# Two-layer metaformer block: the combine, norm and transposes of the routed experts done by halves of the tokens, and the last slot's Gelu in two parts

## The chip, the cores and the metric

The kernel runs on one core of a Trainium2 chip. All data are fp32. The metric is the device time of one execution in microseconds; the time of a version is the median of its runs. A profile is one further execution, recorded by the hardware.

The engines are named as in the profile: PE does matmuls (PEld loads their weights), DVE does vector operations, ACT does activations (it has to load a table set before a function that the present set lacks), POOL does vector operations and the indirect DMAs, SP issues most DMAs. Each engine works through its own queue in the order that was fixed when the kernel was built.

## The reference

The input x has 4 batches of 384 channels and 32 x 32 positions (1024 tokens). Two layers follow each other, each with a convolution-like part and a token part:

```
x = x + scan_block(ln_c(x))            # selective scan in 4 directions, norm, gelu
t = tokens(x)
t = t + experts(ln_t(t))               # 4 experts, top 2 per token:
                                       #   scores -> softmax -> top 2, weights masked / sum
                                       #   h = gelu(x @ w1[e] + b1[e]);  y = h @ w2[e] + b2[e]
                                       #   out = sum over the two experts of weight * y
x = from_tokens(t)
x = x + attention(ln_c(x))             # 8 heads of 64, q = k = v = one projection
t = tokens(x)
t = t + ffn(ln_t(t))                   # Kronecker weights, gelu
```

The change touches the gelu of the experts, the sum `t + out`, and the norm `ln_c` (mean and variance over the 384 channels of each token, eps 1e-6) with which the attention begins.

## The kernel before, in words

`build` runs the scan layer for batches 0 to 3. When batch b of the scan is traced, `between` traces the "tail" of batch b - 1: routing, experts, attention and the last layers. So tails 0 to 2 share the engines with the scan of later batches; the tail of batch 3 comes last, with the tail of batch 2 finishing beside its experts. From its attention on, batch 3 is alone.

The order of work on each engine isn't written out by hand. The framework traces the program, gives each instruction a priority by its place in the program, and fills each engine's queue in a simulated time: at each moment the ready instruction with the best priority. A block under `high_priority(offset=FORWARD)` (FORWARD = 20000) is moved that far forward; `combine` and `prologue` stand in such a block, `experts` and `attention` don't. `depend` adds a dependency by hand, `issue_after` keeps an instruction behind another on its engine. Buffers are handed out by tags with a fixed number of slots: in PSUM, tag "p" has 3 banks and tag "o" has 1 in all stages up to the attention of batch 3, which has 6 and 2.

**Scan.** Per unit of 512 tokens and 128 channels, POOL multiplies (L440, L468), ACT takes the exponential (L449, into PSUM), DVE scans (L454) and multiplies (L461), PE sums over states (L475). SP loads its operands (`dtr` L424, `bcs` L350). For batches after the first POOL has L395 and L396 as well.

**Experts.** The 2048 (token, expert) rows of a batch lie sorted by expert in 11 slots: 8 of 256 rows, 3 of 128. Per slot the rows are transposed (L924), h is made in chunks of one PSUM bank (L941; in a slot of 128 rows a chunk holds 4 of the 12 blocks of 128 hidden units), ACT moves each block to `hs` with its bias (L946, Identity), then one Gelu works on the whole of `hs` in place (L949) and `exp_again` puts the log/exp table set back behind it (L148). PE multiplies by w2 (L956, `y_ps` in bank "o"), DVE adds the bias (L960), a DMA writes the rows (L963; for the last slot on ACT's queue). Each fp32 matmul appears in the profile as two records, a transpose as one.

**Combine.** `xt` (the residual tokens, 8 blocks of 128) is loaded. POOL makes two diagonal matrices of the gate weights (L977) and issues 16 indirect DMAs (L986), two per token block, that fetch the two experts' rows into `got[m]`. For each block PE multiplies by the diagonals (L993, `w_ps` in bank "p") and DVE adds the sum to `xt` (L996). One SP DMA stores `xt` (L997).

**Prologue.** `stats` takes each block's mean and variance on DVE (L543, L544); after all eight, ACT makes the inverse root as exp(-0.5 ln(var + eps)) (L152, L153), copies it to a PSUM bank of tag "p" (L552), DVE makes `less` = -mean * rstd (L553), ACT writes the normed blocks over `got[m]` (L1009, eight). Then, for each half of the tokens and each of 3 channel chunks, PE transposes four blocks into one bank "p" (L1017) and ACT copies it to `xc` (L1021).

**Attention.** Per pair of heads, `project` loads weights (L1035), multiplies by `xc` in two halves of 512 tokens (L1042, copies L1045) and transposes (L1051, copies L1054). Scores (L1065), exponentials (L1071) and their products (L1111) follow in steps of 128 by 512.

Of the kernel before, what the change touches and what calls it, by code (L numbers as in the profile page):

```python
# [11 lines left out]
AF = mybir.ActivationFunctionType  # L12
# [5 lines left out]
P = 128  # L18
B = 4
D = 384  # L20
DC = D // P
HW = 32
L = HW * HW
HF = 512
NH = L // HF
# [12 lines left out]
FC = HID // P  # L38
# [7 lines left out]
NSLOT = NFULL + NHALF  # L46
# [5 lines left out]
MB = L // P  # L52
# [63 lines left out]
class Body:  # L116
# [389 lines left out]
    def first_layer(self, b, room):  # L506

        self.experts(b, self.slots, room)
        with self.tc.high_priority(offset=FORWARD):
            xt, xn = self.combine(b, *self.place, room)  # L510
            return self.prologue(xt, xn, room)

    def second_layer(self, b, xc, room, between):
        att = self.attention(xc, self.sums[:, b], room)
# [18 lines left out]

        return self.x2[b].rearrange("(m p) d -> p m d", p=P)

    def stats(self, xt, eps, room):

        nc = self.nc
        st = room.tile([P, MB, 6], "st", "st")
        mv = room.tile([P, MB, 2], "mv", "mv")  # L540
        rstd = room.tile([P, MB], "rstd", "rstd")
        for m in range(MB):
            nc.vector.bn_stats(st[:, m, :], xt[:, m, :])  # L543
            nc.vector.bn_aggr(mv[:, m, :], st[:, m, :])  # L544
        self.inverse_root(rstd, mv[:, :, 1], eps)
        return mv[:, :, 0], rstd

    def less_mean(self, mean, rstd, room, tag):

        less = room.tile([P, MB], tag, "less")  # L550
        ps = room.bank("p", "less_ps")[:, :MB]
        self.nc.scalar.copy(ps, rstd)  # L552
        self.nc.vector.scalar_tensor_tensor(less, mean, -1.0, ps, op0=ALU.mult, op1=ALU.mult)  # L553
        return less
# [316 lines left out]
    def experts(self, b, routed, room):  # L871
# [60 lines left out]
        for s in range(NSLOT):  # L932
            w1, w2, bb = weights
            at, size = extent(s)
            hs = room.tile([P, FC, size], "k12", "hs")
            n = HF // size
            for f in range(0, FC, n):
                ps = room.bank("p", "h_ps").rearrange("p (r l) -> p r l", l=size)
                for r in range(n):
                    for c in range(DC):  # L940
                        nc.tensor.matmul(  # L941
                            ps[:, r, :], w1[(f + r) // wf][:, c, (f + r) % wf * P : ((f + r) % wf + 1) * P],
                            xc[:, c, :], start=(c == 0), stop=(c == DC - 1),
                        )
                for r in range(n):
                    nc.scalar.activation(  # L946
                        hs[:, f + r, :], ps[:, r, :], AF.Identity, bias=bb[:, f + r : f + r + 1]
                    )
            self.exp_again(nc.scalar.activation(hs, hs, AF.Gelu).ins)  # L949
            if s + 1 < NSLOT:  # L950
                weights, xc = fetch(s + 1), gather(s + 1)
            y = room.tile([P, size // P, D], "k4", "y")
            for t in range(size // P):
                out = room.bank("o", "y_ps")
                for f in range(FC):
                    nc.tensor.matmul(  # L956
                        out[:, :D], hs[:, f, t * P : (t + 1) * P], w2[f // wf][:, f % wf, :],
                        start=(f == 0), stop=(f == FC - 1),
                    )
                nc.vector.tensor_add(y[:, t, :], out[:, :D], bb[:, FC:])  # L960

            queue = nc.sync if s + 1 < NSLOT else nc.scalar
            queue.dma_start(  # L963
                out=made[at : at + size, :].rearrange("(t p) d -> p t d", p=P), in_=y
            )

    def combine(self, b, pos, gate, room):


        nc = self.nc  # L970
# [12 lines left out]
        for m in range(MB):  # L983
            got.append(room.tile([P, TOP, D], "kw", "got"))
            for k in range(TOP):
# [1 line left out]
                    out=got[m][:, k, :], out_offset=None, in_=self.made[b][:, :],  # L987
                    in_offset=bass.IndirectOffsetOnAxis(ap=pos[:, k, m : m + 1], axis=0),
                )
        for m in range(MB):  # L990
            ps = room.bank("p", "w_ps")[:, :D]
            for k in range(TOP):
                nc.tensor.matmul(  # L993
                    ps, diag[k][:, m, :], got[m][:, k, :], start=(k == 0), stop=(k == TOP - 1)
                )
            nc.vector.tensor_add(xt[:, m, :], xt[:, m, :], ps)  # L996
        nc.sync.dma_start(out=self.tokens(b), in_=xt)  # L997
        return xt, [got[m][:, 0, :] for m in range(MB)]

    def prologue(self, xt, xn, room):


        nc = self.nc
        mean, rstd = self.stats(xt, self.eps6, room)
        less = self.less_mean(mean, rstd, room, "less")
        for m in range(MB):
            nc.scalar.activation(  # L1009
                xn[m], xt[:, m, :], AF.Identity, bias=less[:, m : m + 1], scale=rstd[:, m : m + 1]  # L1010
            )
        xc = room.tile([P, DC, L], "k12", "xc")
        for i in range(NH):
            for c in range(DC):
                ps = room.bank("p", "tc_ps")
                for j in range(HF // P):
                    nc.tensor.transpose(  # L1017
                        ps[:, j * P : (j + 1) * P], xn[i * (HF // P) + j][:, c * P : (c + 1) * P],
                        self.ident,
                    )  # L1020
                nc.scalar.copy(xc[:, c, halves(i)], ps)  # L1021
        return xc
# [452 lines left out]
```

## Time and profile before

| | |
|---|---|
| median of 3 runs | 4278.92 us (4278.86 to 4291.83) |
| the profiled execution's own time | 4300.74 us |
| its span, first to last instruction | 4299.0 us |
| mean granted clock of PE | 0.865 |
| busy: PE, DVE, ACT, POOL | 77%, 66%, 59%, 70% |
| last slot's Gelu of batch 3, start | 3968.94 us |
| gathers of batch 3, first and last issue | 3983.42 and 4004.11 us |
| first w_ps of batch 3's attention | 4017.40 us |

A row of the timeline gives the start in us from the span's start, the duration of the group in us, the engine, the line of the kernel, the operation, what it writes and reads, how many instructions are merged, and in brackets the idle time before it with what ended it. A row of the table of stretches gives start and end, length, the busy time of PE, PEld, DVE, ACT and POOL in that stretch with the number of instructions, PE's granted clock (1.00 is full speed), the share of the DMA engines that was busy, and GB/s.

### The profile page before, as it was taken

Reading aid. Unit: us, or ns where it says so; the run is one execution under the profiler, and the core shown is the slowest. Engines: PE = TensorE matmul, PEld = TensorE weight load, DVE = VectorE, ACT = ScalarE, POOL = GpSimd, SP = SyncE. Lnnn points to the kernel's source line nnn. Section 1 sums busy time; section 2 is a strip of 40 time slices with the busy share of each in tenths; the row PEclk is TensorE's granted clock in tenths of the full one; section 3 lists DMA queues with packets and bytes.
Section 4 is the critical chain, followed back from the end, with each engine's and each line's share of the span. In section 5 each row is a group of like instructions: output and inputs, shape, how many; then the busy total and the mean of one; then the engine's idle time right before and its main releaser. Section 6 shows DMA issues by size and latency. Waiting matters only on the chain. (4 is left out here: it accounts for less than half of the span.)

```text
span 4299.0 us, 45575 instructions
## 1 busy us (share of the span) xinstructions
PE 3329.5 (77%) x13244; PEld 1560.8 (36%) x13244; DVE 2852.0 (66%) x4200; ACT 2516.4 (59%) x4486; POOL 3020.0 (70%) x1471
## 2 busy tenths in 40 slices
PE   6445444389897888589985889579896889998896
PEld 2111111155553223145652223135553225566322
DVE  5998997878786867788786878878887820010101
ACT  5555545556665775666664777666665654343354
POOL 5999997898898968789898978888989810000100
PEclk8666666689998999589997999679998999999997
DMA  5454563577795535578886434558789243345100
GB/s 140 128 124 122 135 170 107 168 220 224 229 276 158 137 113 142 169 207 236 239 257 191 114 101 140 158 173 237 234 236 272 77 158 100 121 143 202 50 26 19
DMA packets 410322, 693.69 MB, mean 161 GB/s; under 512 B 51024, under 2 KB 209616, under 8 KB 410064
## 3 DMA queue, kind: packets, MB, share of 16 engines
q1 hardware_dynamic: 400752, 664.29, 53.4%
q0 software_dynamic: 8192, 25.17, 1.8%
q8 instruction: 106, 1.74, 0.2%
q14 instruction: 152, 1.25, 0.1%
q10 hardware_dynamic: 1120, 1.25, 0.1%
HBM read 569.00 MB, written 121.50 MB: 161 GB/s over the span
## 5 line engine op out<-in xcount | busy, mean ns | idle before, releaser
L440 POOL TENSOR_TENSOR bx<-dtr,bcs 128x1024 f32<-128x1024 f32 x768 | 1791.8, 2358 | 181.1 <-PE acc L475 93.6
L449 ACT ACTIVATE da<-dtr,nega 128x512 f32<-128x512 f32 x1536 | 1045.5, 690 | 928.7 <-DVE bx L461 580.8
L468 POOL TENSOR_TENSOR bx<-bx,bcs 128x1024 f32<-128x1024 f32 x384 | 903.7, 2357 | 154.6 <-DVE carry L465 67.3
L475 PE MATMUL acc<-bx,sel 128*32 128x512 f32 x3072 | 493.5, 701 | 306.4 <-POOL bx L468 261.0
L941 PE MATMUL h_ps<-xc,w 128*128 128x256 f32 (+1 forms) x3168 | 663.5, 365 | 47.7 <-DVE xc L928 17.4
L956 PE MATMUL y_ps<-w,hs 128*128 128x384 f32 x1824 | 644.6, 507 | 52.5 <-ACT hs L949 52.5
L941 PEld LDWEIGHTS h_ps<-xc,w 128*128 128x128 f32 x3168 | 551.2, 198 | 218.9 <-issue 93.7
L454 DVE TENSOR_TENSOR_SCAN bx<-da,carry,bx 128x512 f32<-128x512 f32 x384 | 473.8, 1270 | 114.7 <-ACT da L449 64.4
L454 DVE TENSOR_TENSOR_SCAN da<-da,carry,bx 128x512 f32<-128x512 f32 x384 | 476.1, 1273 | 77.5 <-ACT da L449 62.1
L454 DVE TENSOR_TENSOR_SCAN bx<-da,bx 128x512 f32<-128x512 f32 x384 | 453.7, 1211 | 90.9 <-ACT da L449 54.3
L461 DVE TENSOR_TENSOR bx<-da,bcs 128x512 f32<-128x512 f32 x768 | 509.8, 679 | 3.0
L454 DVE TENSOR_TENSOR_SCAN da<-da,bx 128x512 f32<-128x512 f32 x384 | 455.5, 1219 | 76.5 <-ACT da L449 53.0
L956 PEld LDWEIGHTS y_ps<-w,hs 128*128 128x128 f32 x1824 | 353.0, 197 | 337.4 <-issue 71.7
L1071 ACT ACTIVATE ex<-s_ps 128x512 f32<-128x512 f32 x512 | 300.3, 591 | 164.2 <-PE s_ps L1065 148.4
L1065 PE MATMUL s_ps<-w 64*128 64x512 f32 x1024 | 305.1, 659 | 68.5 <-ACT ex L1071 64.4
L977 POOL TENSOR_TENSOR diag<-ident,g_weight 128x1024 f32<-128x1024 f32 x8 | 15.1, 1903 | 443.1 <-PE xc_ps L924 430.0
L1111 PE MATMUL o_acc<-ex,vt 128*64 128x512 f32 x1024 | 286.1, 638 | 24.6 <-ACT ex L1071 18.5
L946 ACT ACTIVATE hs<-h_ps,bb 128x256 f32<-128x256 f32 (+1 forms) x528 | 199.9, 440 | 174.9 <-PE h_ps L941 170.9
L475 PEld LDWEIGHTS acc<-bx,sel 128*32 128x32 f32 x3072 | 76.2, 116 | 603.9 <-POOL bx L468 373.3
L960 DVE TENSOR_TENSOR y<-y_ps,bb 128x384 f32<-128x384 f32 x76 | 41.6, 548 | 250.6 <-PE y_ps L956 250.6
L365 PE MATMUL dt_ps<-xd,wdt 108*128 108x512 f32 x192 | 123.6, 731 | 73.0 <-ACT mag L404 48.3
L1065 PEld LDWEIGHTS s_ps<-w 64*128 64x128 f32 x1024 | 81.8, 189 | 269.1 <-ACT ex L1071 222.6
(218 smaller groups left out, 3593.3 us busy)
## 6 DMA issues: line engine op xcount, KB each, us to landing
w<-in_w SPq DMA_DIRECT2D x352, 576.0 KB
dtr<-dd SPq DMA_DIRECT2D x1536, 128.0 KB
bcs<-both SPq DMA_DIRECT2D x512, 128.0 KB
dd<-one_e SPq DMA_DIRECT2D x96, 256.0 KB
dd<-mag SPq DMA_DIRECT2D x96, 256.0 KB
rows<-zero SPq DMA_DIRECT2D x76, 192.0 KB
xt<-x SPq DMA_DIRECT2D x32, 384.0 KB
xs<-rows SPq DMA_DIRECT2D x32, 384.0 KB
```

Of the source, the lines that this page charges most:

```text
L440: pool = nc.gpsimd.tensor_mul(bx, dtr[q][1], bc[:, 0].unsqueeze(1).to_broadcast([P, 2, HF])).ins
L449: nc.scalar.activation(da, dtr[q][0][:, j, :], AF.Exp, scale=nega[:, col : col + 1])
L454: nc.vector.tensor_tensor_scan(run(h), run(da), run(bx[:, j, :]), 0.0 if first else hold, ALU.mult, ALU.add,)
L461: dve = nc.vector.tensor_mul(bx[:, j, :], h, cg).ins
L468: pool = nc.gpsimd.tensor_mul(bx, bx, cg.unsqueeze(1).to_broadcast([P, 2, HF])).ins
L475: nc.tensor.matmul(acc[lo : lo + DB, :], sel, out[q][:, j, :], start=(g == 0), stop=(g == NG - 1),)
L941: nc.tensor.matmul(ps[:, r, :], w1[(f + r) // wf][:, c, (f + r) % wf * P : ((f + r) % wf + 1) * P], xc[:, c, :], start=(c == 0), stop=(c = ...
L946: nc.scalar.activation(hs[:, f + r, :], ps[:, r, :], AF.Identity, bias=bb[:, f + r : f + r + 1])
L956: nc.tensor.matmul(out[:, :D], hs[:, f, t * P : (t + 1) * P], w2[f // wf][:, f % wf, :], start=(f == 0), stop=(f == FC - 1),)
L1065: ins = nc.tensor.matmul(ps, w[rows, j * P : (j + 1) * P], w[rows, halves(i)], start=True, stop=True).ins
L1071: done.append(nc.scalar.activation(ex[:, o, :], ps, AF.Exp, scale=HD**-0.5, accum_out=sums[:, t, 2 * j + o, i : i + 1],).ins)
L1111: ins = nc.tensor.matmul(out[cols, :], made[t][1][:, j, cols], ex[:, o, :], start=(j == 0), stop=(j == MB - 1),).ins
```

## The change

- **Combine.** The loop over token blocks becomes an inner function `add(m)`, which `combine` returns. The store of `xt` becomes two DMAs, each for four blocks, issued behind blocks 3 and 7.
- **Prologue.** It runs over the two halves. For each half: `add(m)`, statistics of four blocks; inverse root, `less` (for four columns, through the bank "o" in place of "p"); four normed blocks; then the transposes and copies of this half. `xc` is taken from its pool after the first half's norms. `stats` goes away. Another caller, `second_layer_exact`, passes no `add`; it runs only if a guard on the attention's sums is hit.
- **Last slot of the experts.** When PE has done the first matmul of the last block of the last chunk, one Gelu works in place on the 8 blocks of `hs` that the chunks before have filled (it has a hand-made dependency on that matmul). The four blocks of the last chunk go from PSUM through Gelu with their bias straight to `hs`, with no Identity. `exp_again` follows the last of them. Other slots stay as they are.

```diff
@@ -507,8 +507,8 @@
 
         self.experts(b, self.slots, room)
         with self.tc.high_priority(offset=FORWARD):
-            xt, xn = self.combine(b, *self.place, room)
-            return self.prologue(xt, xn, room)
+            xt, xn, add = self.combine(b, *self.place, room)
+            return self.prologue(xt, xn, room, add)
 
     def second_layer(self, b, xc, room, between):
         att = self.attention(xc, self.sums[:, b], room)
@@ -533,22 +533,11 @@
 
         return self.x2[b].rearrange("(m p) d -> p m d", p=P)
 
-    def stats(self, xt, eps, room):
-
-        nc = self.nc
-        st = room.tile([P, MB, 6], "st", "st")
-        mv = room.tile([P, MB, 2], "mv", "mv")
-        rstd = room.tile([P, MB], "rstd", "rstd")
-        for m in range(MB):
-            nc.vector.bn_stats(st[:, m, :], xt[:, m, :])
-            nc.vector.bn_aggr(mv[:, m, :], st[:, m, :])
-        self.inverse_root(rstd, mv[:, :, 1], eps)
-        return mv[:, :, 0], rstd
-
-    def less_mean(self, mean, rstd, room, tag):
-
-        less = room.tile([P, MB], tag, "less")
-        ps = room.bank("p", "less_ps")[:, :MB]
+    def less_mean(self, mean, rstd, room, tag, bank="p"):
+
+        n = rstd.shape[-1]
+        less = room.tile([P, n], tag, "less")
+        ps = room.bank(bank, "less_ps")[:, :n]
         self.nc.scalar.copy(ps, rstd)
         self.nc.vector.scalar_tensor_tensor(less, mean, -1.0, ps, op0=ALU.mult, op1=ALU.mult)
         return less
@@ -935,18 +924,25 @@
             hs = room.tile([P, FC, size], "k12", "hs")
             n = HF // size
             for f in range(0, FC, n):
+                last = s == NSLOT - 1 and f == FC - n
                 ps = room.bank("p", "h_ps").rearrange("p (r l) -> p r l", l=size)
                 for r in range(n):
                     for c in range(DC):
-                        nc.tensor.matmul(
+                        ins = nc.tensor.matmul(
                             ps[:, r, :], w1[(f + r) // wf][:, c, (f + r) % wf * P : ((f + r) % wf + 1) * P],
                             xc[:, c, :], start=(c == 0), stop=(c == DC - 1),
-                        )
+                        ).ins
+                        if last and r == n - 1 and c == 0:
+                            wide = nc.scalar.activation(hs[:, :f, :], hs[:, :f, :], AF.Gelu).ins
+                            self.depend(wide, ins)
                 for r in range(n):
-                    nc.scalar.activation(
-                        hs[:, f + r, :], ps[:, r, :], AF.Identity, bias=bb[:, f + r : f + r + 1]
-                    )
-            self.exp_again(nc.scalar.activation(hs, hs, AF.Gelu).ins)
+                    done = nc.scalar.activation(
+                        hs[:, f + r, :], ps[:, r, :], AF.Gelu if last else AF.Identity,
+                        bias=bb[:, f + r : f + r + 1],
+                    ).ins
+            if not last:
+                done = nc.scalar.activation(hs, hs, AF.Gelu).ins
+            self.exp_again(done)
             if s + 1 < NSLOT:
                 weights, xc = fetch(s + 1), gather(s + 1)
             y = room.tile([P, size // P, D], "k4", "y")
@@ -987,30 +983,45 @@
                     out=got[m][:, k, :], out_offset=None, in_=self.made[b][:, :],
                     in_offset=bass.IndirectOffsetOnAxis(ap=pos[:, k, m : m + 1], axis=0),
                 )
-        for m in range(MB):
+        def add(m):
             ps = room.bank("p", "w_ps")[:, :D]
             for k in range(TOP):
                 nc.tensor.matmul(
                     ps, diag[k][:, m, :], got[m][:, k, :], start=(k == 0), stop=(k == TOP - 1)
                 )
             nc.vector.tensor_add(xt[:, m, :], xt[:, m, :], ps)
-        nc.sync.dma_start(out=self.tokens(b), in_=xt)
-        return xt, [got[m][:, 0, :] for m in range(MB)]
-
-
-
-    def prologue(self, xt, xn, room):
+            if m % (MB // NH) == MB // NH - 1:
+                part = slice(m + 1 - MB // NH, m + 1)
+                nc.sync.dma_start(out=self.tokens(b)[:, part, :], in_=xt[:, part, :])
+
+        return xt, [got[m][:, 0, :] for m in range(MB)], add
+
+
+
+    def prologue(self, xt, xn, room, add=lambda m: None):
 
 
         nc = self.nc
-        mean, rstd = self.stats(xt, self.eps6, room)
-        less = self.less_mean(mean, rstd, room, "less")
-        for m in range(MB):
-            nc.scalar.activation(
-                xn[m], xt[:, m, :], AF.Identity, bias=less[:, m : m + 1], scale=rstd[:, m : m + 1]
-            )
-        xc = room.tile([P, DC, L], "k12", "xc")
+        nh = MB // NH
+        xc = None
         for i in range(NH):
+            st = room.tile([P, nh, 6], f"st{i}", "st")
+            mv = room.tile([P, nh, 2], f"mv{i}", "mv")
+            rstd = room.tile([P, nh], f"rstd{i}", "rstd")
+            for j in range(nh):
+                m = i * nh + j
+                add(m)
+                nc.vector.bn_stats(st[:, j, :], xt[:, m, :])
+                nc.vector.bn_aggr(mv[:, j, :], st[:, j, :])
+            self.inverse_root(rstd, mv[:, :, 1], self.eps6)
+            less = self.less_mean(mv[:, :, 0], rstd, room, f"less{i}", "o")
+            for j in range(nh):
+                m = i * nh + j
+                nc.scalar.activation(
+                    xn[m], xt[:, m, :], AF.Identity, bias=less[:, j : j + 1], scale=rstd[:, j : j + 1]
+                )
+            if xc is None:
+                xc = room.tile([P, DC, L], "k12", "xc")
             for c in range(DC):
                 ps = room.bank("p", "tc_ps")
                 for j in range(HF // P):
```

## The prediction

> **What bounds the kernel now.** I read the granted clock first (0.865 over the 4299.0 us span), then the table of stretches, then the timeline of the one place that the change touches without cover, last the chain that ended last and POOL's waits.
>
> ```profile
> 806.00:3445.00 2639.00, 2154.76 (x8935) 1061.28 (x8933) 2078.62 (x3015) 1716.11 (x3035) 2252.08 (x1098) 0.89 0.65 189
> 3445.00:3966.00 521.00, 494.58 (x2056) 287.57 (x2056) 54.77 (x160) 221.70 (x430) 22.27 (x21) 0.98 0.44 148
> 3966.00:4024.00 58.00, 36.41 (x106) 18.34 (x105) 11.10 (x26) 15.29 (x27) 16.10 (x17) 0.85 0.28 86
> 4024.00:4299.00 275.00, 238.08 (x943) 78.39 (x942) 19.56 (x37) 136.49 (x329) 0.00 (x0) 0.92 0.06 19
> ```
> Columns: stretch, length, busy us of PE, PEld, DVE, ACT and POOL, granted clock, DMA share, GB/s. From 806 to 3445 the scan of one batch and the experts of another share the engines: POOL is busy 85%, PE 82%, nobody is alone. From 3445 to 3966 (rest of batch 2, experts of batch 3) PE is busy 95%. From 3966 to 4024 PE is busy 63%: the end of the last slot, the combine and the prologue of batch 3, with no other work left. After that the attention holds PE; the chain that ended last alternates there between L1065 and L1111. So a microsecond taken from 3966 to 4024 is a microsecond of the time. The same code runs three times more under the scan (last slot, combine, prologue near 1290 to 1358, 2270 to 2328, 3290 to 3355), where it counts only through the other engines.
>
> The uncovered place, by its timeline (start, us, engine, line, count, idle before):
> ```profile
> 3966.48 1.14 ACT L946 ACTIVATE hs<-h_ps,bb 128x128 f32<-128x128 f32 x4 [1.54 <-PE h_ps L941]
> 3967.64 1.28 ACT L949 ACT_TABLE_LOAD   x1
> 3968.94 1.48 ACT L949 ACTIVATE hs<-hs 128x1536 f32<-128x1536 f32 x1
> 3970.47 9.57 PE L956 MATMUL y_ps<-w,hs 128*128 128x384 f32 x24 [4.03 <-ACT hs L949]
> ...
> 4009.30 0.18 DVE L544 BATCH_NORM_AGGREGATE mv<-st 128x2 f32<-128x6 f32 x1
> 4009.51 0.30 ACT L152 ACTIVATE rstd<-mv,eps 128x8 f32<-128x8 f32 x1 [37.80 <-DVE mv L544]
> 4010.54 4.89 ACT L1009 ACTIVATE got<-xt,less,rstd 128x384 f32<-128x384 f32 x8 [0.28 <-DVE less L553]
> 4011.30 2.82 PE L1017 MATMUL tc_ps<-ident,got 128*128 128x128 f32 x12 [3.22 <-ACT got L1009]
> 4015.33 2.96 ACT L1021 COPY xc<-tc_ps 128x512 f32<-128x512 f32 x6
> 4015.95 1.62 PE L1017 MATMUL tc_ps<-ident,got 128*128 128x128 f32 x12 [1.83 <-ACT xc L1021]
> 4017.40 5.32 PE L1042 MATMUL w_ps<-xc,wqkv 128*128 128x512 f32 x12
> ```
> Two stalls: PE idles 4.03 us for the last Gelu; and no norm starts before the eighth token block has its statistics, although ACT had waited 37.8 us. Between them lie the gathers (16 issues on POOL, 1.257 us apart), which set when each block can be added; nothing in the change moves their pace.
>
> **Last slot's Gelu (part A).** Before: four Identities 1.14, table load 1.28, Gelu of 1536 elements 1.48: PE waits from 3966.45 to 3970.47. After: the first 8 of 12 blocks get their own Gelu. From the two L949 forms (3072 elements 2.763 us, 1536 in 1.482) one element costs 0.83 ns and the start 0.20 us, so 1024 elements cost 1.05 us. It waits for a matmul four records before the last: h_ps runs at 4.41/38 = 0.116 us per record, so that one ends at 3966.45 - 0.46 = 3965.99. The table load fits the 1.54 us in which ACT waits for PE anyway, if the wait sits on the Gelu; if the load waits too, it costs 1.28. Wide Gelu 3966.26 to 3967.31, PE starts at 3967.34: 3.1 us sooner (1.85 if the load waits). The four Gelus from PSUM (1.14, as the Identities) end at 3968.45, under the eight y_ps blocks that need only the wide part (16 records of 0.33 us, 5.3 us). The shorter idle has a second effect, which the table of stretches shows:
> ```profile
> 3970.40:3973.70 3.30, 3.23 (x5) 1.85 (x6) 0.00 (x0) 1.30 (x2) 0.00 (x0) 0.51 0.00 0
> 4014.10:4015.90 1.80, 0.02 (x1) 0.00 (x0) 0.00 (x0) 1.80 (x5) 0.00 (x0) 0.85 0.00 0
> 4015.90:4017.40 1.50, 1.45 (x12) 1.33 (x13) 0.00 (x0) 1.50 (x4) 0.00 (x0) 1.00 0.00 0
> ```
> After 4.0 us of idle PE restarts at clock 0.51; after 1.8 us it restarts at 1.00. With an idle of 0.9 us (at most 2.2) y_ps takes 24 x 0.33 = 7.9 instead of 9.57: 1.7 us. Part A: **4.8 us**, low end 3.5.
>
> **Halves (part B), batch 3.** Small instructions added: one more Ln, Exp, copy and less (0.30 + 0.21 + 0.17 + 0.16), all for the first half, at a time when ACT and DVE wait for gathers; the one SP store becomes two of 0.38 us issue, and SP has nothing behind it until 4022.75. The less of the first half makes DVE wait 0.8 us with the adds of blocks 4 to 7 behind it; these come every 2.5 us and cost 1.3, so it is absorbed. Second half: last statistics end at 4009.48 as before, norms start at 4010.54, but four instead of eight: at (4.89 - 0.69)/7 = 0.60 apart the last ends at 4010.54 + 1.80 + 0.69 = 4013.03 (was 4015.43). One transpose (0.135) and one copy (0.58) later, at 4013.85, the second half of w_ps can start; copies two and three (0.475 apart) stay ahead of it. The first half's 12 transposes, 3 copies and 6 of the 12 records of w_ps are done before, in PE's waits (3.22 + 1.83, and those between gathers); its first weights were loaded long before. So w_ps ends at 4013.85 + 6 x 0.443 = 4016.5 instead of 4022.72: **6.2 us**. Low end, 3.0: the queue of PE holds w_ps behind all transposes. Or the 12 first transposes stand ahead of the w_ps of block 4: they end near 4004.6, and blocks 4 to 7 follow at DVE's pace, the last add 1.6 us later: 4.6. High end, 11: v_ps and w_ps of the next head pair (0.6 + 2.7, and a score) fill PE's waits too.
>
> **Batches 0 to 2.** During the 16 gathers POOL does nothing else, and ACT, DVE and PE mostly wait (ACT 20.7 us before L152 at 1347). Moving half of the norms into that time relieves ACT afterwards, but POOL then had work without a gap to 1370, 2340 and 3345. The earlier Gelu hands ACT back to the scan about 2.1 us sooner per batch (ends -6.3 in all); against it stand the new PE and DVE waits in queues that the scan shares. I take 0, with ends -6 and +24 (below).
>
> A rule of the Trainium skill speaks against part A: "ScalarE: Activation LUTs", Table sets, asks to batch activations by table set, since every switch costs some 2.7 us; splitting the Gelu opens a gap into which an Exp of the scan can slip. The trace has that case, at the Gelus of the scan's end:
> ```profile
> 665.90 1.52 ACT L230 ACTIVATE y<-y,cols 128x512 f32<-128x512 f32 x2
> 667.44 1.28 ACT L153 ACT_TABLE_LOAD   x1
> 668.73 0.58 ACT L153 ACTIVATE ln_var<-ln_var 128x512 f32<-128x512 f32 x1
> 669.33 1.28 ACT L230 ACT_TABLE_LOAD   x1
> ```
> Two loads of 1.28 with the next instruction right behind: 2.6 us for each of three batches, 7.7 of ACT at most; by the page, an estimate of 5.3 each, 16. I use the trace's. ACT is busy 65% in that stage, so the wait of POOL behind it, not the sum, would be paid. Batch 3 has no scan and is free of it.
>
> **Sum.** 4.8 + 6.2 + 0 = 11.0 us. The profiled execution took 4300.74 us (span 4299.0, 1.7 around it), so 4289.7 there; it lay 21.8 above the median of 4278.92, and the saved work scales hardly at all, so **4267.9**.
>
> **Rivals.**
> 1. More than forecast: PE's waits take the next pair's work as well (+4.8) and the ACT time freed under the scan reaches POOL (6.3): 4257. For it: project(1) is next in program order and POOL loses 35.4 us to ACT L382. Against: POOL is fully fed right behind each combine.
> 2. The change doesn't do what it says: the planner keeps the first half's transposes and w_ps behind the last block, and its wide Gelu late. Only four fewer norms stay (2.4) with part of A: near 4275. Against: PE's order follows readiness in the planner's simulated time, and in that it has a gap too.
> 3. Slower: under the scan PE's queue now holds transposes that wait for norms, inside the run of gathers and ahead of the L475 matmuls; bx is then released late and POOL stalls. The kind of wait exists:
> ```profile
> POOL bx L440 <- PE acc L475: 83.3, 22, 16.2
> ```
> Single waits reach 16.2 us. It decides from 11.0/3 = 3.7 us per batch; at 8 each, 4278.9 - 11.0 + 24 = 4292. Against: PE was idle in those waits already.
>
> **How the numbers follow.** 0.3% (12.8 us) is about what a measurement of this kernel can tell from no change. Forecast 50%, within 4263 to 4273 (14 of it below 4266.1, faster by over 0.3%; 36 within). Rival 1: 26%, faster. Rival 2: 9%, same. Rival 3: 15%, 13 slower by over 0.3%, 2 same. So faster 0.40, same 0.47, slower 0.13. The range 4254 to 4290 leaves out about 7% below and 9% above.
>
> **What would show it.** A: PE's idle ahead of the last y_ps in batch 3 falls from 4.03 to about 0.9 and the clock behind it stays at 1.00; a load from the log/exp set between the two Gelus of one of batches 0 to 2 shows the skill's rule at work. B: eight norms in two groups of four with the first before the last gather; six w_ps records before the last transposes; last statistics to end of w_ps 7 us instead of 13.2. Wrong if POOL's waits for PE acc between 806 and 3445 grow beyond 83.3 by more than 11, or if the scan ends away from 3445 by more than a few us, since every instruction's place is planned anew.

## The result

The changed kernel takes 4267.69 us (median of 7 runs, 4263.45 to 4277.06), the kernel before 4289.97 in 7 runs beside it (4278.86 to 4292.33; the three shown first are among these). The ratio is 0.9957, 95% interval 0.9942 to 0.9971: about 18 us less, 0.43%. (The two medians are 22.3 us apart, the two means 18.6.) Forecast were 4267.9 us and 11 us less. The number came out; most of the gain did not come from where the forecast has it. "us less" below is the ratio's distance from 1, times 4290, so that experiments made on different chips stand on one scale.

The profiled execution of the changed kernel (4267.69 us, span 4265.9, clock 0.866) against the one shown of before. First the same four stretches, cut at the same events (columns: stretch, length, busy us of PE, PEld, DVE, ACT and POOL, granted clock, DMA share, GB/s):

```profile
799.00:3423.00 2624.00, 2143.28 (x8951) 1060.38 (x8953) 2085.59 (x3015) 1719.87 (x3052) 2251.24 (x1098) 0.89 0.64 190
3423.00:3933.80 510.80, 491.92 (x2041) 288.26 (x2037) 57.27 (x163) 219.93 (x423) 22.76 (x21) 0.98 0.45 151
3933.80:3987.30 53.50, 35.77 (x103) 18.80 (x102) 10.95 (x27) 15.42 (x30) 15.62 (x17) 0.84 0.30 93
3987.30:4265.90 278.60, 241.92 (x943) 79.23 (x942) 19.57 (x37) 136.48 (x329) 0.00 (x0) 0.90 0.06 19
```

The uncovered place of batch 3, third row, went from 57.53 us (3966.45 to 4023.98) to 53.45: 4.1 us where the forecast had 11. The first two rows together are 25 us shorter (2639 + 521 to 2624 + 510.8), where the forecast had nothing; 7 of the 32 us by which the place begins earlier were there before batch 1's scan, at the end of the first stretch of the trace (806 to 799), where both kernels run the same instructions. The last row is 3.6 us longer, with the same instructions. So one pair of executions carries differences of several us that are not the change's.

The timeline of the uncovered place after the change, in the columns of the forecast's second fence:

```profile
3931.17 1.14 ACT L939 ACTIVATE hs<-h_ps,bb 128x128 f32<-128x128 f32 x4 [7.97 <-PE h_ps L931]
3933.45 1.28 ACT L936 ACT_TABLE_LOAD   x1 [1.14 <-PE h_ps L931]
3934.74 1.06 ACT L936 ACTIVATE hs<-hs 128x1024 f32<-128x1024 f32 x1
3935.85 8.01 PE L952 MATMUL y_ps<-w,hs 128*128 128x384 f32 x24 [2.04 <-ACT hs L936]
...
3962.37 12.24 SPq L995 DMA_DIRECT2D x<-xt  x2
3964.20 2.50 ACT L1020 ACTIVATE got<-xt,less,rstd 128x384 f32<-128x384 f32 x4 [0.28 <-DVE less L542]
3964.96 2.82 PE L1028 MATMUL tc_ps<-ident,got 128*128 128x128 f32 x12 [3.21 <-ACT got L1020]
3968.03 5.59 PE L989 MATMUL w_ps<-got,diag 128*128 128x384 f32 x16 [0.25 <-ACT xc L1032]
3974.84 0.18 DVE L1015 BATCH_NORM_AGGREGATE mv<-st 128x2 f32<-128x6 f32 x1
3976.82 2.70 PE L1028 MATMUL tc_ps<-ident,got 128*128 128x128 f32 x12 [3.20 <-ACT got L1020]
3979.31 6.68 PE L1053 MATMUL w_ps<-xc,wqkv 128*128 128x512 f32 x12
```

Three things are to be seen. The table load does not start at 3932.31, when the last Identity had ended, but 1.14 us later, when the matmul that its Gelu waits for was done: it waits with the Gelu. (The wait stands on ACT's queue as an instruction of its own, ahead of the load.) All 16 records of the sums of blocks 4 to 7 (L989) stand behind the first half's 12 transposes (L1028). And all 12 records of the attention's w_ps (L1053) stand behind the second half's transposes; nothing of the attention begins early.

POOL's waits under the scan, from 799 to 3423 (waiting line, releaser: us, times, longest):

```profile
POOL bx L440 <- PE acc L475: 102.1, 33, 15.2
POOL bx L468 <- DVE bx L454: 47.3, 23, 7.3
POOL bx L468 <- DVE carry L465: 43.4, 24, 6.5
```

The wait for PE, 83.3 us before, has grown by 18.8, which the forecast named as a sign that it would be wrong. But all of POOL's waits from 806 to the end of the scan together fell from 374.9 to 360.2 us: POOL waits more for PE and less for others.

### The profile page after: what moved, and what is told of

Its sections match the earlier page's. It is cut to its first block, busy times and chain, and to the rows that moved or that the text cites. A ratio compares the mean times of both kernels' runs of the same rounds, so it can differ in the third digit from the quotient of the medians.

```text
span 4265.9 us, 45621 instructions
## 1 busy us (share of the span) xinstructions
PE 3317.7 (78%) x13244; PEld 1560.6 (37%) x13244; DVE 2863.1 (67%) x4204; ACT 2518.3 (59%) x4498; POOL 3019.6 (71%) x1471
## 5 line engine op out<-in xcount | busy, mean ns | idle before, releaser
L952 PE MATMUL y_ps<-w,hs 128*128 128x384 f32 x1824 | 634.1, 500 | 35.0 <-ACT hs L944 26.6
```

The lines of the kernel that those rows point to most:

```text
L952: nc.tensor.matmul(out[:, :D], hs[:, f, t * P : (t + 1) * P], w2[f // wf][:, f % wf, :], start=(f == 0), stop=(f == FC - 1),)
```

## The experiments

All of these compute the whole of the reference. Five of them need batch 3 to differ from the others; there the functions exist twice, and `b` selects. The planner lays out every queue anew for each build. How far two orders differ is counted here on PE's records in the two traces: like instructions in a row are one run, and a run counts as moved when it has no partner in the other trace's sequence. Before's trace has 1732 runs. (The row counts in the expectations were taken in another, finer way and count both sides of each difference.)

### Which batch gains: the last, or the first three

Both parts of the change in batch 3 alone (`combine_h` and `prologue_h` are the changed functions), so that the queues ahead of it are those of the kernel before (no run of PE or POOL moved up to batch 3's combine):

```diff
+            if b == B - 1:
+                xt, xn, add = self.combine_h(b, *self.place, room)
+                return self.prologue_h(xt, xn, room, add)
...
+                last = b == B - 1 and s == NSLOT - 1 and f == FC - n
```

> Both parts for batch 3 alone; batches 0 to 2 as before, and the queues of the engines up to batch 3's last slot are those of before. The traces of before and after show what the uncovered place gained: the idle ahead of the last y_ps fell from 4.03 to 2.04 us and y_ps took 8.01 instead of 9.57 (part A 3.6), and from the last gather's end to the end of w_ps it went from 17.7 to 17.2 (part B 0.4). So my reading now is 4.0 us less than before. If the forecast's sum for this place is right after all (4.8 + 6.2), it is 11 us less. If the whole gain of the change comes from here, 18 us less.

Measured 0.9993 (0.9983 to 1.0003): 3 us less. The other half of the change, `b < B - 1` in the same two places:

> Both parts for batches 0 to 2 alone; batch 3 as before. Theory 1 (the planner lays the queues anew and happens to do better) and theory 2 (the halves and the earlier Gelu relieve the scan) both expect the rest of the gain here: 18 - 4 = 14 us less than before. The forecast took 0 for these batches.

Measured 0.9941 (0.9927 to 0.9956): 25 us less. So the gain lies in batches 0 to 2, which the forecast took at 0, and batch 3 by itself gives 3 us with an interval that includes nothing.

### Does the order move the time without the change

The kernel before, with its one store of `xt` split in two behind the last block. No computation differs, but from batch 0's combine on (1350 us) the planner then lays PE's queue otherwise: some 620 of its 1732 runs moved:

```diff
-        nc.sync.dma_start(out=self.tokens(b), in_=xt)
+        for part in (slice(0, MB // NH), slice(MB // NH, MB)):
+            nc.sync.dma_start(out=self.tokens(b)[:, part, :], in_=xt[:, part, :])
```

> The kernel before with one edit that does next to nothing: combine's store of xt goes in two DMAs, both after the last block, in all batches. Work added: four issues of 0.38 us on SP. Theory 2 expects no change, within 2 us. Theory 1 expects that this alone has the planner lay the queues of batches 0 to 2 anew and that the time moves by 5 to 20 us, in either direction, with the differences between 800 and 3440 us of the trace.

Measured 1.0071 (1.0053 to 1.0089): 30 us more. One added DMA per batch cost more than the whole change gained. "Both after the last block" holds for the program's text only: each part waits for its own four blocks alone, and in batch 3 the first went out 18.6 us after the end of y_ps, among the gathers.

The same store in four parts (some 65 runs moved, all from batch 2's combine on):

```diff
+        for m in range(0, MB, 2):
+            nc.sync.dma_start(out=self.tokens(b)[:, m : m + 2, :], in_=xt[:, m : m + 2, :])
```

> The kernel before with its x<-xt store in four DMAs behind the last block instead of one. No computation differs; the planner lays 194 rows of TensorE's queue otherwise (two DMAs gave about 1000 rows and 30 us). Theory 1 (order): 3 to 30 us from the kernel before, either way, less than the two DMAs gave if fewer moved rows mean fewer chances. Theory 2 (the issues and the packets of the split store themselves cost): slower than with two DMAs, by 30 to 60 us.

Measured 1.0018 (1.0006 to 1.003): 8 us more. Four DMAs cost less than two, so it isn't the number of DMAs that costs; what goes with the 30 us is the moved order.

The changed kernel, with its store in four parts, one behind every second block (some 280 runs moved, against the changed kernel's 1744):

```diff
-            if m % (MB // NH) == MB // NH - 1:
-                part = slice(m + 1 - MB // NH, m + 1)
+            if m % 2 == 1:
+                part = slice(m - 1, m + 1)
```

> The changed kernel with the store of x<-xt in four DMAs, one behind every second block, instead of two. No computation differs, but the planner lays about 700 rows of TensorE's queue otherwise. Where the store's place alone was changed with all other queues kept, the time stood within 2 us of the changed kernel's. Theory 1 (the gain of batches 0 to 2 belongs to the order that the planner fell into): the time parts from the changed kernel's by 5 us or more, either way. Theory 2 (it belongs to the work by halves): within 4 us of the changed kernel, so 14 to 22 below the kernel before.

Measured 1.0064 (1.0048 to 1.008): 27 us more than before, 46 more than the changed kernel. All of the change's gain in batches 0 to 2 is gone, with the work by halves still there. That is the plainest answer of the study: the work by halves does not bring the gain by itself; with another order of the queues it is gone.

One place where POOL stands is longer in both slow orders. POOL's waits around batch 1's combine and the scan beside it, 2200 to 2600 us, in the kernel before with two stores:

```profile
POOL bx L440 <- PE acc L475: 33.1, 4, 23.2
```

and in the changed kernel with four:

```profile
POOL bx L440 <- issue: 28.4, 3, 22.1
```

One stall of 22 to 23 us each, near 2500 us. ("issue" is time in which nothing that the profile shows was waited for.) The same stall is in the kernel before with 16.2 us (2503) and in the changed one with 14.3 (2462), so it makes 6 to 9 us of the difference; the rest is spread over many waits.

### The two parts, each in all batches

Only the Gelu in two parts (some 330 runs of PE moved, from batch 1's combine on), then only the halves (some 660, from batch 0's):

> The last slot's Gelu in two parts in all batches; sums, norms, transposes and the store as in the kernel before. In batch 3 this is worth 3.5 us by the changed kernel's trace (1.99 shorter idle, 1.56 of clock). In batches 0 to 2 the planner lays about 640 rows of TensorE's queue otherwise, from the end of batch 0 on. Theory 1 (the order that the planner falls into moves the time, whatever the edit): the total is anywhere from 30 us slower to 25 faster, and the trace shows it as POOL's progress through the scan parting from the kernel before at batches 1 to 2, with waits for acc, y or bx grown or shrunk there. Theory 2 (the gain of batches 0 to 2 comes from Gelus that finish earlier): 12 to 25 us faster, with POOL ahead from each batch's last Gelu on.

> Sums, norms, transposes and the store by halves in all batches, the Gelu as in the kernel before. In batch 3 this is worth about 0.4 us by the changed kernel's trace. In batches 0 to 2 about 1050 rows of TensorE's queue are laid otherwise. The change gave 18 us and the Gelu's part alone 2. Theory 1 (the order decides, and no part of the change has its own price in batches 0 to 2): any value from 25 us faster to 30 slower, and the two parts' own gains do not add up to the 18. Theory 2 (the halves are what gained): 14 to 18 us faster, so that with the Gelu's 2 they make the change's 18.

Measured 0.9995 (0.9986 to 1.0005), 2 us less, and 1.0025 (1.001 to 1.0039), 11 us more. Together the parts gave 18 us less; one by one they make 9 more. No price per part can be read from that in batches 0 to 2. In batch 3 the traces add up within 1 us: from the last h_ps to the first score it takes 54.06 us with the Gelu alone (3.47 less than before), 57.66 with the halves alone (0.13 more), and 53.45 with both (4.08 less). But the same code in batch 3 alone took 55.47, for a reason that the section on the hardware shows.

### Batch 3 with the order that the forecast assumed

The change in batch 3 alone once more, with the Gelu's table asked for ahead of its wait, and PE's queue told what the forecast had taken for granted: first half's transposes behind block 5's sum, the first half of the attention's first w_ps behind block 7's, then the second half's transposes. (`done` is the last Identity of the chunk before; `hold` is the matmul behind which the next transposes queue; `first` makes that half of w_ps.)

```diff
+                if last and b == B - 1:
+                    with self.tc.issue_after(done):
+                        nc.scalar.preload_act_table_set("gelu_and_others")
...
+        sums(0)
+        xc = room.tile([P, DC, L], "k12", "xc")
+        sums(1)
+        hold = [self.adds[5]]
+        turn(0)
+        got = first(xc)
+        hold = [got[-1]]
+        turn(1)
```

> As last_only, with the two things mended that cost the forecast its sum in batch 3: the Gelu table set is loaded behind the Identities of the chunk before, and PE's queue has the first half's transposes behind block 5's sum, then, behind block 7's, the first half of w_ps, then the second half's transposes. If the forecast's mechanism was right and only the planner's order was wrong: idle ahead of y_ps 0.9 us, last statistics to end of w_ps 7 us, 11 us less than before. If the places don't pay for another reason (clock, banks), no better than last_only, 4 us less.

Measured 0.9962 (0.9947 to 0.9976): 16 us less. Its timeline:

```profile
3946.81 1.28 ACT L962 ACT_TABLE_LOAD   x1
3948.10 1.06 ACT L971 ACTIVATE hs<-hs 128x1024 f32<-128x1024 f32 x1
3949.21 8.01 PE L987 MATMUL y_ps<-w,hs 128*128 128x384 f32 x24 [0.92 <-ACT hs L971]
...
3975.85 15.58 SPq L1098 DMA_DIRECT2D x<-xt  x2
3983.62 5.49 PE L1092 MATMUL w_ps<-got,diag 128*128 128x384 f32 x8 [4.29 <-DMA got<-made,g_pos]
```

The table load now runs behind the chunk's Identities, PE's idle is 0.92 us and y_ps takes 8.01: part A gives 3.11 + 1.56 = 4.67 us. From the last statistics (3991.84) to the end of the attention's w_ps (3999.24) it takes 7.4 us, against 13.24 before. But PE waits 4.29 us for rows, right after the first half's store went out at 3975.85. The texts on record name block 6; by the count of records, 22 of the 32 stand before this row, so that it is the second expert's rows of block 5, whose gather was issued 0.4 us behind the store.

Is that store to blame? The same kernel with batch 3's store in one DMA at the end, all other queues kept:

```diff
+            if b == B - 1 and m == MB - 1:
+                nc.sync.dma_start(out=self.tokens(b), in_=xt)
+            if b < B - 1 and m % (MB // NH) == MB // NH - 1:
```

> last_fixed with one edit: batch 3's x<-xt store goes out in one DMA behind the sum of block 7 (as in the kernel before) instead of two, the first of them behind block 3. Every other queue is that of last_fixed. Theory 1 (the first half's store of 0.79 MB runs among the last gathers and holds them back): TensorE's wait for got of block 6, 4.29 us in last_fixed, falls to about what the kernel before had there (under 1.5), the sums of blocks 6 and 7 end 2 to 4 us earlier after y_ps, and the time is 2 to 4 us below last_fixed's, so 18 to 20 us below the kernel before by last_fixed's 16. Theory 2 (the gathers of block 6 were late by themselves): the wait stays at 3 to 4.3 us and the time with it, within 1 us of last_fixed.

Measured 0.9976 (0.9966 to 0.9986): 10 us less, so not better than with the early store. The wait in its timeline, though, is gone; the longest for a block is now this one:

```profile
3977.01 0.88 PE L1092 MATMUL w_ps<-got,diag 128*128 128x384 f32 x2 [1.61 <-DMA got<-made,g_pos]
```

Since the two readings disagree, the kernel with the early store was run again:

> last_fixed once more, unchanged, since its time (16 us below the kernel before, 8 runs) and last_late's (10 below, 17 runs) stand in the other order than their traces, where last_late's batch 3 is 3.7 us shorter. Theory 1 (the collision of store and gathers is real and the first median was a lucky one): 7 to 9 us below the kernel before. Theory 2 (the early store is worth its collision for a reason that the traces have not shown): 14 to 18 below again. The trace should again show TensorE waiting some 4 us for got of block 6.

Measured 0.9981 (0.997 to 0.9991): 8 us less, and in this execution the row in question is

```profile
3993.53 4.54 PE L1092 MATMUL w_ps<-got,diag 128*128 128x384 f32 x8 [2.40 <-issue]
```

The uncovered place took 52.22 us in the first execution with the early store, 49.18 in the second, 48.53 with the late one. So the collision costs between 0.7 and 3.7 us in these traces and nothing that the times can tell. Both expectations were too sharp; that a half store among the gathers costs the kernel several us is not shown. The wait itself does follow the store: PE waits for the second rows of block 5 for 4.29 and 2.40 us in these two executions and 1.96 in the kernel before with two stores, and for 0.34 in the kernel before, 0.32 here with the late store and 0.28 in the version with both gains below.

The store's place was also moved in the changed kernel itself:

```diff
-            if m % (MB // NH) == MB // NH - 1:
-                part = slice(m + 1 - MB // NH, m + 1)
-                nc.sync.dma_start(out=self.tokens(b)[:, part, :], in_=xt[:, part, :])
+            if m == MB - 1:
+                for part in (slice(0, MB // NH), slice(MB // NH, MB)):
+                    nc.sync.dma_start(out=self.tokens(b)[:, part, :], in_=xt[:, part, :])
```

> The changed kernel with one edit: both half stores of x<-xt go out behind block 7 in every batch. All queues but SP's are those of the changed kernel, so this is the place of the store alone. Theory 1 (the half store among the gathers holds them and the loads of the scan back by 2 to 4 us a batch, and only batch 3 lies open): 1 to 4 us below the changed kernel, 19 to 22 below the kernel before. Theory 2 (the earlier store of batches 0 to 2 frees SP's queue and was part of the 14 us gained there): 5 to 14 us above the changed kernel.

Measured 0.9952 (0.9936 to 0.9968): 21 us less, as the changed kernel. For batch 3 this was no test: with SP's queue empty, the first store still went out at 3961.61, 26.6 us after y_ps began, as in the changed kernel (26.5), since it waits only for its own four blocks. It serves as a repeat of the changed kernel.

### Both gains together

The changed kernel's batches 0 to 2 with the mended batch 3 and its one late store:

> The change in all batches, its batches 0 to 2 as they stand in the changed kernel, and batch 3 as in last_late (table asked for ahead, the order on TensorE written out, one store). Queues ahead of batch 3 are those of the changed kernel and of early_only. Theory 1 (two gains that add: the queues of batches 0 to 2 as re-planned give what early_only gave, 25 us, and the mended batch 3 gives 12 to 19): 37 to 44 us below the kernel before. Theory 2 (early_only's gain was used up where the batches overlap, so that batch 3's does not add): 20 to 28 us below. The trace should show an idle of 0.9 us ahead of the last y_ps and about 7 us from the last statistics to the end of the attention's w_ps.

Measured 0.9922 (0.9906 to 0.9939), 4253.94 us: 33 us less than before, the best of all versions. It lies between the two expectations, and is about what the two halves measured apart: 25 (batches 0 to 2) and 10 (the mended batch 3). In its trace the uncovered place takes 47.28 us, 10.25 less than in the trace of before.

### All traces side by side

Per profiled execution: the end of POOL's part of the scan, POOL's waits from 806 us to there, the end of the last h_ps of batch 3, the length of the uncovered place (to the first score), and the rest of the span. (The stretches above are cut 11 us behind the end of the scan as it is taken here.)

```
                    less by   scan end  POOL waits  last h_ps  place    rest
queues of before, up to batch 3
  before              -        3434.2     374.9      3966.45   57.53   275.0
  batch 3 alone       3        3421.6     363.4      3943.91   55.47   278.7
  mended, run 1      16        3418.8     364.5      3948.29   52.22   276.6
  mended, run 2       8        3423.7     365.8      3960.04   49.18   272.9
  mended, late store 10        3409.7     353.0      3940.95   48.53   276.8
queues of the changed kernel, up to batch 3
  after              18        3412.0     360.2      3933.81   53.45   278.6
  after, two late    21        3409.0     354.2      3932.99   53.52   279.1
  batches 0 to 2     25        3400.9     347.7      3925.25   60.32   278.7
  both gains         33        3408.9     357.8      3930.30   47.28   274.9
other orders
  Gelu alone          2        3425.4     366.5      3942.20   54.06   274.6
  halves alone      -11        3448.0     391.9      3978.23   57.66   274.8
  before, 4 stores   -8        3441.8     382.8      3980.09   60.90   278.3
  after, 4 stores   -27        3462.1     408.4      3988.86   54.88   274.4
  before, 2 stores  -30        3468.2     412.8      3992.75   60.75   275.0
```

Up to the last h_ps the nine executions of the first two groups fall into two bands that don't overlap: 3941 to 3966 (mean 3951.9) and 3925 to 3934 (mean 3930.6). The distance of the means, 21.3 us, is what the order in batches 0 to 2 is worth by these traces (33, 21 and 9 us between traces taken side by side); 13.9 of it are there when the scan ends, the rest comes while batch 2 finishes beside batch 3's experts. The scan's end follows POOL's waits nearly one to one over all fourteen rows: from 347.7 to 412.8 us of waits (65), from 3400.9 to 3468.2 (67). That is bookkeeping, since POOL is busy for 2250 to 2252 us from 806 to there in all of them: the sum of its waits tells where time goes, and not why.

Where the order helps can be read from POOL's progress. Until batch 0's combine the means of the two bands lie within 5 us; behind it, from POOL's 468th scan product to its 576th, the changed kernel's order gains 18.8 us on average, and behind batch 1's, from the 756th to the 864th, another 23.5, which puts it 39.4 us ahead. By the end of the scan 25.5 of these are given back. Against the mean of the first band slower orders are ahead at the 576th product too, the halves alone by 17 us, the kernel before with two stores by 11 and the changed one with four by 14, the last two behind by 3 and 4 at the 648th; so no single place makes an order good. The second gain by POOL's waits, before (2209 to 2569):

```profile
POOL bx L440 <- PE acc L475: 19.9, 3, 16.2
POOL x L237 <- ACT y L230: 11.8, 2, 9.4
POOL bx L440 <- DMA dtr<-dd: 11.5, 2, 5.9
POOL bx L468 <- DVE bx L454: 10.3, 4, 5.1
```

and after (2194 to 2530):

```profile
POOL bx L440 <- PE acc L475: 22.5, 4, 14.3
POOL x L237 <- ACT y L230: 7.4, 1, 7.4
...
POOL bx L468 <- DVE bx L454: 3.1, 2, 2.4
```

The stretch is 24 us shorter, and POOL's waits in it fell from 63.3 to 41.3. Half of that is the wait for `dtr`, which went to nothing: in SP's queue of before, 4 loads of `bcs` stand between the store of `xt` and 19 DMAs for the routing (rows<-zero, 12.85 us of issue), in that of the changed kernel 8 of them and 4 of `dtr`. Given back it is from 2530 to 3412, where the wait for PE rose from 14.3 to 27.1 and one of 10.4 for the DMA of `out` came in. Which rows of the order do this was not tested one by one.

## Why the prediction was right in its number and wrong in its reasons

**What bounds the kernel.** Right for the one place it was drawn for: what was taken from batch 3's 58 us came off the time, as far as the runs can tell (25 us less without it, 33 with it). Incomplete for the rest. "Nobody is alone" under the scan is true of busy shares, but the stretch held 375 us of POOL's waits that an order can lengthen or shorten, and the forecast put no size on that.

**Batches 0 to 2.** This is the step that failed: "I take 0, with ends -6 and +24". The changed kernel's order gained 21 us by the traces, 25 by the time of the version that has it in these batches alone. The step priced the work that moves (a Gelu handed back 2.1 us sooner, norms done earlier) and put the planning anew only among the signs that would make it wrong. A neutral store cost 30 us, and a neutral edit of the changed kernel cost 46: the spread of orders is about four times the sum that was forecast. Why the changed kernel's order is the better one stays open: the traces show where POOL's waits differ, and no run shows which moved instruction makes the difference.

**Part A.** 4.8 us forecast, 3.55 measured in the changed kernel: 1.99 of shorter idle (4.03 to 2.04) and 1.56 of clock (9.57 to 8.01). This is the stated low end, and its stated reason: the load waits with the Gelu. The full clock after 2.04 us of idle was in part luck: one execution of five did not have it. With the table asked for ahead, idle 0.92 (forecast 0.9) and 4.67 us (forecast 4.8).

**Part B, batch 3.** 6.2 us forecast, 0.5 measured. Two low ends were given as alternatives and came together. The first half's transposes stand ahead of blocks 4 to 7, so that the last statistics come 31.2 us after the end of y_ps, in place of 29.4 (1.7 later; 1.6 was given). All of w_ps stands behind all transposes, and its 12 records took 6.68 us for 5.32 (granted clock 0.79 against 1.00), so that statistics to end of w_ps fell from 13.24 to 10.97 only. Left over: 2.27 - 1.72. With the order written out, 7.4 us (forecast 7), and the whole place 8.4 to 10.3 us shorter in three of four executions, 5.3 in the first one with the early store; forecast 11. The 7 us held, and the whole place came near its 11; that the planner would choose this order was the error, and rival 2 had the reason in it. (The forecast's own sum gives 4013.75 where it has 4013.85; and its 4.8 and 2.4 for rival 2 would give 4271.7, so that "near 4275" takes most of part A away without saying so.)

**The store.** Counted as two issues with nothing behind them. Its packets among the gathers were left out; the traces put that at 0.7 to 3.7 us, the times leave it open. In the changed kernel it is hidden, since the sums of blocks 4 to 7 stand behind the transposes.

**The skill's rule.** No table load slipped between the two Gelus: the line of the wide Gelu has 4 loads, the line of the four Gelus from PSUM none, and with 40 for the other slots there are 44, as before. The 7.7 us of ACT, or the page's estimate of 16, were not paid.

**Rivals.** The change was worth less than rival 1 has, and not by its mechanism, since no pair's work moved into PE's waits. Rival 3's wait came (PE acc from 83.3 to 102.1), and its sign did not: POOL's waits for DVE fell by 30.6 at the same time (145.6 to 115.0). A single wait was the wrong thing to watch. By its own signs the forecast was wrong. Its number is luck, two errors against each other: it started from the median of three runs, 11 us below that of seven, and the medians then fell by 22.3 us where it expected 11 (18, so 7 more than forecast, by the ratio).

## What to carry to other kernels

Where a planner lays out the queues, price an edit at two levels: the place where it stands uncovered, from the trace; and the new order of everything else, which has to be measured with neutral edits (here 8 to 46 us for a split store) before a gain of 0.4% is put down to the edit. If a stall is to be filled by work that becomes ready sooner, read or write out the order on that engine; being ready doesn't put it there. Under shared engines a single wait can grow while the time falls, so add up all waits of the busiest engine, and take the sum as a place to look and not as a cause.

## What the hardware showed

**A table load waits with its activation.** ACT was free at 3932.31, and the load started at 3933.45, when the matmul that the Gelu waits for was done. As an instruction of its own behind the Identities it ran during the wait, and PE's idle ahead of y_ps was 0.92 in all four executions.

**The clock after an idle PE.** The forecast had 1.00 for an idle of up to 2.2 us. With 4.03 us of idle y_ps took 9.56 to 9.70 us in five of five executions, with 0.92 us 8.01 in four of four. With 2.04 it was 8.01 in four and 9.70 in one, the change in batch 3 alone:

```profile
3945.95 9.70 PE L966 MATMUL y_ps<-w,hs 128*128 128x384 f32 x24 [2.04 <-ACT hs L950]
```

The traces show why. In all fourteen, every change of the granted clock lies on a grid with steps of 3.41 us. Cut on that grid, the stretches of that execution are

```profile
3943.12:3946.53 3.41, 1.37 (x10) 1.05 (x9) 0.00 (x0) 2.97 (x5) 1.58 (x1) 1.00 0.00 0
3946.53:3949.95 3.42, 3.42 (x7) 1.70 (x6) 0.00 (x0) 1.68 (x3) 0.00 (x0) 0.50 0.00 0
```

and those of the changed kernel

```profile
3930.86:3934.28 3.42, 2.95 (x27) 2.76 (x25) 0.00 (x0) 1.97 (x5) 1.90 (x1) 1.00 0.16 58
3934.28:3937.69 3.41, 1.84 (x6) 1.18 (x7) 0.00 (x0) 3.38 (x7) 0.00 (x0) 1.00 0.00 0
3937.69:3941.10 3.41, 3.41 (x12) 1.97 (x11) 0.00 (x0) 0.44 (x1) 0.00 (x0) 1.00 0.00 0
```

In the first the whole idle of 2.04 us fell into one step (PE busy 1.37 of 3.41), and the next step ran at half the clock. In the other four a border of the grid cut the idle, at most 1.71 us of it lay in one step, and the clock stayed. With 4.03 us of idle one step always held at least 3.31 of it. So in these traces the place of the idle on the grid decides. The Trainium skill, "TensorE: Matmul & The Clock Gate", section "Part 1: The HAM clock gate", has a free-running window of about 3.4 us as well, but gives an idle window as the condition of the slow state; here a window idle for 2.04 us of its 3.41 was enough.

**The same instructions, 4 us apart.** From the first score on all versions do the same work, yet it takes 272.9 to 279.1 us. In the traces of before and after the first 220 us of it agree within 0.1 us of busy PE per stretch of 20; then they part. Before, in the table of stretches:

```profile
4264.00:4284.00 20.00, 8.33 (x36) 1.86 (x38) 0.00 (x0) 15.94 (x16) 0.00 (x0) 0.67 0.00 0
```

and the changed kernel, as far behind its first score:

```profile
4227.30:4247.30 20.00, 10.19 (x30) 2.09 (x28) 0.00 (x0) 12.82 (x15) 0.00 (x0) 0.51 0.00 0
```

PE is busy about half the time there, and the granted clock is 0.67 in one execution and 0.51 in the other; that the grid's phase parts them is likely, but was not worked out step by step. The uncovered place does it too: with the code of before in batch 3 it took 57.53 us in one execution and 60.32 in another (batches 0 to 2 changed), where the 12 records of w_ps took 6.89 us in place of 5.32, at a granted clock of 0.77 in place of 1.00. A difference of 3 us between two traces is within that. So the gains of the place that are counted above from 57.53 would each be 2.8 us larger from the other trace.
